# The last pair of a pipelined graph kernel: transposing by TensorE instead of by way of DRAM, a softmax per graph, and own space for y and v

## The chip, the cores and the metric

The kernel runs on one NeuronCore of one Trainium2 chip. The metric is the device time of one execution in microseconds (us). Lengths inside an execution come from the trace of one profiled execution per kernel.

Names of engines in the profile: PE is TensorE (PEld its loads of weights), DVE is VectorE, ACT is ScalarE, POOL is GpSimd, SP is the engine that issues most transfers (883 of 1525 in the trace before).

## The reference

128 graphs of 128 nodes with 512 features, all in fp32, pass through two layers. Cut to what matters:

```python
h = jnp.maximum(_layernorm(x), 0.0)
x = x + _L0_gnn_ref(h, adj, ...)           # layer 0: attention over adj, three hops
h = jnp.maximum(_layernorm(x), 0.0)        # this is "h2" in the kernel
q, k = jnp.split(h @ Wqk, 2, axis=-1)
v = h @ Wv
agg = jnp.einsum('bij,bjd->bid', adj, k * mask)
w = mask / sqrt(512) * jnp.einsum('bid,bid->bi', q, agg)
x = x + jax.nn.softmax(w, axis=1)[:, :, None] * v      # softmax over a graph's nodes
```

The kernel folds Wqk into one matrix, so that layer 1 computes y = h2 times a matrix, v = h2 Wv, agg = adj h2 and the score of a node as the sum of y times agg.

## The kernel before

The graphs are taken in 64 pairs, as a software pipeline: while layer 0 of pair p runs, layer 1 of pair p-1 follows it. Each layer multiplies by a two-by-two block scheme with seven products instead of eight (hence "first to seventh product"; in layer 1 they are run in the order 1, 6, 7, 5, 2, 3, 4, and I call them by their place in that order only where I say so). The products take h2 transposed. The kernel gets that by a trip through DRAM: it stores h2, reads it back by blocks, and lets VectorE transpose blocks of 32 by 32. This is hidden behind the products of other pairs but for two waits of TensorE: 3.29 us for an early pair (at 100.26 us) and 10.45 us for the last.

```python
def by_blocks(h):
    hd = dram.tile([G, P, D], FP, name="hd")
    nc.sync.dma_start(hd.rearrange("g n d -> n g d"), h)
    hv = front.tile([P, G, Q, P], FP, name="hv")
    ...                                   # four loads, one for each 32 partitions
    return hv

def transposed(hv, dst):
    for j in range(G):
        nc.vector.transpose(dst[:, j]..., hv[:, j]...)

def strassen1(p, ahead):                  # layer 1's products of pair p
    product = products(SX2.pop(p), R1)
    yv = late["p"].tile([P, G, 2, 2, HD], FP, name="yv")      # one buffer
    o = ...                               # o[j][nh]: half nh of graph j, y and v side by side
    s = late["p"].tile([P, 3, D], FP, name="s1")
    a, b, c = (ps_m.tile([P, D], FP, name="pm") for _ in range(3))
    product(a, 1, True)
    nc.scalar.copy(s[:, 0], a)
    product(b, 6, True)
    nc.vector.tensor_add(s[:, 1], b, s[:, 0])
    product(c, 7, True)
    agg = [aggregate(p, 0)]
    product(b, 5, False)
    nc.vector.tensor_add(s[:, 2], b, s[:, 0])
    nc.vector.tensor_add(o[1][1], c, s[:, 2])
    ...
    product(a, 2, False)
    nc.scalar.copy(o[0][0], a)
    agg.append(aggregate(p, 1))
    product(b, 3, False)
    nc.vector.tensor_add(o[0][1], b, s[:, 0])
    product(c, 4, False)
    nc.vector.tensor_add(o[1][0], c, s[:, 1])
    return yv, scores(p, yv, agg)         # a score per node, both graphs

def finish(peak, p, yv, ws, pw):          # softmax and result of a pair
    nc.vector.tensor_reduce(peak, pw, AX.X, OP.max, negate=True)
    ...                                   # exponentials on ScalarE, reciprocal, product
    for j in range(G):
        nc.vector.scalar_tensor_tensor(o, yv[:, j, :, 1, :], w[:, 3, j:j + 1], o, ...)
    nc.sync.dma_start(out[p * G:(p + 1) * G].rearrange("b n d -> n b d"), x1)

for p in range(NP + 1):
    if p < NP:
        ...
        strassen0(p, steps)               # layer 0's products; finishes pair p-2 on the way
    else:
        end()                             # finishes pair NP-2
    ...
    if p < NP:
        H2[p] = norm_relu(X1[p], "h2", late["p"])
        hv2 = by_blocks(H2[p])
    ...
    if p > 0:
        yv, w = strassen1(p - 1, p + 2)
    ...
    if p > 0:                             # scores to all partitions, by way of DRAM but for the last
        ends.append((p - 1, yv, w, spread_pair(w, "pw", p < NP)))
    if p < NP:
        X2[p] = late["p"].tile(...)
        transposed(hv2, X2[p]...)
        SX2[p] = left_sums(...)
end()
```

The order of an engine's instructions in the trace (below, the compiled order) follows the source only roughly: in the trace before, VectorE runs the softmax of the pair before (L461, at 2367.68 us) ahead of the last pair's transposes (L279, at 2370.84 us), which the source writes first.

## Time and profile before

| | before |
|---|---|
| median time | 2400.05 us (2398.68 to 2400.31, 3 runs) |
| span of the profiled execution | 2394.7 us |
| TensorE busy | 98% of the span |
| TensorE's longest wait on a product | 10.45 us, at 2361.15 us |
| mean granted clock from 2371.6 to 2385.6 us | 0.88 |

How to read the page: the share of busy time says which engine sets the time; the row of forty digits says where in the execution that holds. A change of the last of 64 pairs can only act in the last slice, so the rest of the reading is a timeline of that slice: look for the stretch without TensorE, see what ended it, and follow that back. The lines are in the prediction below.

### The profile page before, as it was taken

The numbers are of one execution on the slowest core, as the hardware profiler recorded it, in microseconds if no ns is written. First come the engines' busy times: TensorE is split into PE (matmuls) and PEld (weight loads), VectorE is DVE, ScalarE is ACT, GpSimd is POOL, SyncE is SP. The second block draws the span as 40 slices with busy tenths as digits, with TensorE's granted clock in tenths as the row PEclk, the third lists the DMA queues.
The fourth block names the chain that finished last, engine by engine and source line by source line (L and its number), as shares of the span: only waits on it lengthen the run. The fifth ranks groups of instructions, "written<-read, shape, count | busy, mean of one in ns | idle before, by whom it ended". The sixth has DMA issues, their size and how long they took to land.

```text
span 2394.7 us, 27824 instructions
## 1 busy us (share of the span) xinstructions
PE 2338.7 (98%) x8909; PEld 1656.8 (69%) x8909; DVE 1830.6 (76%) x4958; ACT 635.4 (27%) x1557; POOL 369.7 (15%) x646
## 2 busy tenths in 40 slices
PE   5999999999999999999999999999999999999996
PEld 3676676776776776776776776766766766766763
DVE  5777877877877877878878878778778778778764
ACT  3222222222222222222222223223222222222221
POOL 2011111111111111111111111111111111111100
PEclk9999999999999999999999999999999999999998
DMA  8244343343343343343343343442433443443321
GB/s 227 70 112 112 82 115 102 92 114 103 92 106 105 98 106 103 100 106 100 103 106 100 103 106 86 117 106 82 121 105 81 116 110 83 115 112 82 108 67 49
DMA packets 259300, 245.62 MB, mean 103 GB/s; under 512 B 28560, under 2 KB 184336, under 8 KB 259152
## 3 DMA queue, kind: packets, MB, share of 16 engines
q1 hardware_dynamic: 232624, 216.65, 31.9%
q0 software_dynamic: 22304, 25.09, 5.9%
q10 hardware_dynamic: 4224, 2.10, 0.3%
q8 instruction: 70, 1.15, 0.2%
q14 instruction: 78, 0.64, 0.1%
HBM read 142.93 MB, written 100.79 MB: 102 GB/s over the span
## 4 chain that ended last, share of the span: by engine, by line
PE 86%; DVE 6%; DMA 4%; issue 2%; ACT 1%; POOL 0%; DVEq 0%; SPq 0%; POOLq 0%; ACTq 0%
PE pm L367 72%; PE pt L346 8%; PE pt L442 4%; DMA pwd<-pwt 2%; DMA pw<-pwd 1%; PE pt L334 1%; DVE st L224 1%; PE pm L212 1%; PE pt L330 1%; DVE x L279 1%; DVE x L407 0%; DVE sx L354 0%; DVE sx L353 0%; DVE sx L355 0%; DMA pzd<-pzt 0%
## 5 line engine op out<-in xcount | busy, mean ns | idle before, releaser
L367 PE MATMUL pm<-t,sx 128*128 128x256 f32 x2304 | 507.9, 379 | 1.9 <-DVE sx L354 1.9
L367 PEld LDWEIGHTS pm<-t,sx 128*128 128x128 f32 x2304 | 437.6, 190 | 62.1 <-DVE sx L354 2.7
L367 PE MATMUL pm<-b,x 128*128 128x256 f32 x1536 | 363.0, 379 | 0.0
L367 PE MATMUL pm<-f,sx 128*128 128x512 f32 x768 | 352.9, 595 | 4.8 <-DVE s L421 4.8
L367 PEld LDWEIGHTS pm<-b,x 128*128 128x128 f32 x1536 | 282.2, 190 | 59.6 <-issue 29.7
L290 POOL DMA_DIRECT2D pzd<-pzt x126 | 69.9, 556 | 1443.4 <-DVE pzt L287 1443.2
L367 PEld LDWEIGHTS pm<-f,sx 128*128 128x128 f32 x768 | 145.4, 191 | 191.3 <-issue 159.0
L367 PE MATMUL pm<-e,x 128*128 128x512 f32 x512 | 242.9, 597 | 13.7 <-DVE x L279 13.7
L348 ACT COPY x<-pt 128x512 f32<-128x512 f32 x256 | 147.6, 576 | 356.1 <-PE pt L346 356.1
L346 PE MATMUL pt<-tt,h 128*128 128x256 f32 x1024 | 231.5, 379 | 0.0
L262 DVE SCALAR_TENSOR_TENSOR junk<-h,u_bc 128x512 f32<-128x512 f32 x256 | 177.1, 692 | 64.3 <-ACT h L239 52.9
L346 PEld LDWEIGHTS pt<-tt,h 128*128 128x128 f32 x1024 | 194.5, 190 | 26.9 <-ACT tt L335 0.4
L367 PE MATMUL pm<-b,sx 128*128 128x256 f32 x768 | 176.2, 379 | 0.0
L367 PE MATMUL pm<-t,x 128*128 128x256 f32 x768 | 176.2, 379 | 0.0
L367 PEld LDWEIGHTS pm<-e,x 128*128 128x128 f32 x512 | 97.6, 191 | 110.6 <-issue 90.2
L279 DVE STREAM_TRANSPOSE x<-hv 128x512 f32<-128x512 f32 x256 | 166.3, 687 | 7.5 <-DMA hv<-hd 5.6
L307 ACT ACTIVATE s<-s 128x256 f32<-128x256 f32 x63 | 26.2, 416 | 522.8 <-DVE s L305 522.8
L367 PEld LDWEIGHTS pm<-t,x 128*128 128x128 f32 x768 | 145.9, 190 | 19.8
L367 PEld LDWEIGHTS pm<-b,sx 128*128 128x128 f32 x768 | 145.9, 190 | 19.8
L77 POOL DMA_DIRECT2D agb<-in_adj_dram x256 | 152.9, 602 | 18.1 <-DVE aT L319 7.4
L239 ACT ACTIVATE h<-xg,rs 128x512 f32<-128x512 f32 x128 | 97.2, 806 | 184.2 <-DVE rs L236 184.2
L442 PE MATMUL pt<-h,aT 128*128 128x512 f32 x256 | 130.6, 592 | 0.0
(119 smaller groups left out, 2792.7 us busy)
## 6 DMA issues: line engine op xcount, KB each, us to landing
hd<-h SPq DMA_DIRECT2D x128, 512.0 KB, 3.9
hv<-hd SPq DMA_DIRECT2D x512, 128.0 KB, 5.3
xg<-in_x_dram SPq DMA_DIRECT2D x64, 512.0 KB, 3.6
out_dram<-x SPq DMA_DIRECT2D x64, 512.0 KB, 2.8
ag<-in_adj_dram SPq DMA_DIRECT2D x64, 128.0 KB, 2.9
agb<-in_adj_dram POOLq DMA_DIRECT2D x256, 32.0 KB, 4.5
pz<-pzd POOLq DMA_DIRECT2D x63, 128.0 KB, 5.3
pw<-pwd POOLq DMA_DIRECT2D x63, 128.0 KB, 3.3
```

The source lines that it names most:

```text
L77: nc.gpsimd.dma_start(agb[p][c * S32:(c + 1) * S32].rearrange("p g q i -> p (g q) i"), v[c])
L212: nc.tensor.matmul(pm[c], wt[0][:, c * P:(c + 1) * P], wt[1], start=(o == 0), stop=(o == DC - 1))
L224: nc.vector.bn_stats(st, src[:, j, :])
L239: nc.scalar.activation(h[:, j, :], src[:, j, :], AF.Relu, bias=rs[:, 1, j:j + 1], scale=rs[:, 0, j:j + 1])
L262: nc.vector.scalar_tensor_tensor(junk, h[:, j, :], 1.0, u_bc[:, a, :], op0=OP.mult, op1=OP.mult, accum_out=s[:, a * G + j:a * G + j + 1])
L279: nc.vector.transpose(dst[:, j].rearrange("p f (n b) -> p f n b", n=Q), hv[:, j].rearrange("p n (f a) -> p f n a", f=Q))
L290: nc.gpsimd.dma_start(d[j], t[j::S32])
L307: nc.scalar.activation(ex, z, AF.Exp)
L346: nc.tensor.matmul(pt[:, c].rearrange("p k n -> p (k n)"), h[:, j, at:at + P], tt[:, j].rearrange("p k n -> p (k n)"), start=True, stop=True)
L348: nc.scalar.copy(X[p][:, 1:3, j, kh].rearrange("p k c n -> p c k n"), pt)
L367: nc.tensor.matmul(bank[:, :r.shape[-1]], left[i][:, k, c * P:(c + 1) * P], r, start=(first and at == 0), stop=(at == len(chunks) - 1), sk ...
L442: nc.tensor.matmul(pa, AT[p][:, j, :], H2[p][:, j, :], start=True, stop=True)
```

## The change

Its intent: close the hole in front of the last pair's products, and shorten what follows them. Four things change, all for the last pair alone: h2 is stored with its columns reordered and transposed by TensorE; the softmax of the pair before moves behind the last pair's fourth product in program order (number 5); y and v get a buffer of their own, a freed one of layer 0; scores, softmax and store go graph by graph.

```diff
+    def transposed_by_pe(h, dst):
+        for j in range(G):
+            pt = ps_t.tile([P, DC, P], FP, name="pt")
+            for f in range(Q):
+                nc.tensor.transpose(pt[:, f, :], h[:, j, f * P:(f + 1) * P], ident)
+            (nc.vector.tensor_copy if j else nc.scalar.copy)(dst[:, j], pt)
...
-        yv = late["p"].tile([P, G, 2, 2, HD], FP, name="yv")
+        if p + 1 < NP:
+            yv = late["p"].tile([P, G, 2, 2, HD], FP, name="yv")
+        else:
+            yv = front.tile([P, K, G, 2, HC, N], FP, name="x")[:, :2].rearrange(...)
...
         nc.vector.tensor_add(o[1][1], c, s[:, 2])
...
+        if p == NP - 1:
+            end(s[:, 2, :G])
         product(a, 2, False)
...
         nc.vector.tensor_add(o[0][1], b, s[:, 0])
+        w = cols[3 + p % 3]
+        if p == NP - 1:
+            last(p, yv, w, agg, 0)
         product(c, 4, False)
         nc.vector.tensor_add(o[1][0], c, s[:, 1])
-        return yv, scores(p, yv, agg)
+        if p == NP - 1:
+            last(p, yv, w, agg, 1)
+            return
...
+    def last(p, yv, w, agg, j):
+        score(p, yv, w, agg, j)
+        pw = ps_t.tile([P, DC, P], FP, name="pt")
+        spread(pw[:, j, :], w[:, j:j + 1])
+        finish(small.tile([P, G], FP, name="peak"), p, yv, w, pw[:, :G], slice(j, j + 1))
...
-        else:
-            end()
...
-            H2[p] = norm_relu(X1[p], "h2", late["p"])
-            hv2 = by_blocks(H2[p])
+            H2[p] = norm_relu(X1[p], "h2", late["p"], p == NP - 1)
+            if p + 1 < NP:
+                hv2 = by_blocks(H2[p])
...
-            transposed(hv2, X2[p]...)
+            if p + 1 < NP:
+                transposed(hv2, hT2)
+            else:
+                transposed_by_pe(H2[p], hT2)
```

`end(s[:, 2, :G])` puts the maximum of the moved softmax into a corner of a buffer that the sum before it has just read, which keeps the softmax behind that sum.

More of the change, by code (lines that the diff above doesn't have):

```diff
@@ L216, in score_matrix, with norm_relu @@
                 nc.scalar.copy(e[c // HC, nh][:, c % HC, 0, :], pm[c][:, nh * HD:(nh + 1) * HD])
-    def norm_relu(src, name, pool):
+    def norm_relu(src, name, pool, permuted=False):
         mv = small.tile([P, G, 2], FP, name="mv")
@@ L238, in norm_relu, with unpermuted @@
         for j in range(G):
-            nc.scalar.activation(h[:, j, :], src[:, j, :], AF.Relu,
-                                 bias=rs[:, 1, j:j + 1], scale=rs[:, 0, j:j + 1])
-        return h
+            to, at = h[:, j, :], src[:, j, :]
+            if permuted:
+                to, at = unpermuted(to), at.rearrange("p (c f a) -> p c f a", c=DC, f=Q)
+            nc.scalar.activation(to, at, AF.Relu, bias=rs[:, 1, j:j + 1], scale=rs[:, 0, j:j + 1])
+        return h
+    def unpermuted(h):
+        return h.rearrange("p (f c a) -> p c f a", c=DC, f=Q)
     cols = [const.tile([P, S32], FP, name=f"col{i}") for i in range(6)]
@@ L413, in strassen1 @@
         X2.pop(p)
-        yv = late["p"].tile([P, G, 2, 2, HD], FP, name="yv")
+        if p + 1 < NP:
+            yv = late["p"].tile([P, G, 2, 2, HD], FP, name="yv")
+        else:
+            yv = front.tile([P, K, G, 2, HC, N], FP, name="x")[:, :2].rearrange(
+                "p k g h c n -> p (k g h c n)").rearrange("p (j h k d) -> p j h k d", j=G, h=2, k=2)
         o = [[yv[:, j, nh].rearrange("p k d -> p (k d)") for nh in range(2)] for j in range(G)]
@@ L431, in strassen1 @@
         agg.append(aggregate(p, 1))
-        H2.pop(p), AT.pop(p)
         product(b, 3, False)
         nc.vector.tensor_add(o[0][1], b, s[:, 0])
+        w = cols[3 + p % 3]
+        if p == NP - 1:
+            last(p, yv, w, agg, 0)
         product(c, 4, False)
         nc.vector.tensor_add(o[1][0], c, s[:, 1])
-        return yv, scores(p, yv, agg)
+        if p == NP - 1:
+            last(p, yv, w, agg, 1)
+            return
+        for j in range(G):
+            score(p, yv, w, agg, j)
@@ L439, in aggregate @@
+        return yv, w
+    def last(p, yv, w, agg, j):
+        score(p, yv, w, agg, j)
+        pw = ps_t.tile([P, DC, P], FP, name="pt")
+        spread(pw[:, j, :], w[:, j:j + 1])
+        finish(small.tile([P, G], FP, name="peak"), p, yv, w, pw[:, :G], slice(j, j + 1))
     def aggregate(p, j):
         pa = ps_t.tile([P, D], FP, name="pt")
-        nc.tensor.matmul(pa, AT[p][:, j, :], H2[p][:, j, :], start=True, stop=True)
-        return pa
-    def scores(p, yv, agg):
-        w = cols[3 + p % 3]
-        for j in range(G):
-            junk = front.tile([P, D], FP, name="junk", bufs=1)
-            b = p * G + j
-            nc.vector.scalar_tensor_tensor(
-                junk.rearrange("p (k d) -> p k d", k=2), agg[j].rearrange("p (k d) -> p k d", k=2),
-                wscale[:, b:b + 1], yv[:, j, :, 0, :], op0=OP.mult, op1=OP.mult,
-                accum_out=w[:, j:j + 1])
-        return w
@@ L457, in finish, with score @@
-    def finish(peak, p, yv, ws, pw):
+        to, h2 = pa, H2[p][:, j, :]
+        if p == NP - 1:
+            to, h2 = pa.rearrange("p (c f a) -> p c f a", c=DC, f=Q), unpermuted(h2)
+        nc.tensor.matmul(to, AT[p][:, j, :], h2, start=True, stop=True)
+        return pa
+    def score(p, yv, w, agg, j):
+        junk = front.tile([P, D], FP, name="junk", bufs=1)
+        b = p * G + j
+        nc.vector.scalar_tensor_tensor(
+            junk.rearrange("p (k d) -> p k d", k=2), agg[j].rearrange("p (k d) -> p k d", k=2),
+            wscale[:, b:b + 1], yv[:, j, :, 0, :], op0=OP.mult, op1=OP.mult,
+            accum_out=w[:, j:j + 1])
@@ L460, in finish @@
+    def finish(peak, p, yv, ws, pw, graphs=slice(0, G)):
         w = ws[:, :6 * G].rearrange("p (k g) -> p k g", g=G)
-        nc.vector.tensor_reduce(peak, pw, AX.X, OP.max, negate=True)
-        for j in range(G):
+        js = range(G)[graphs]
+        nc.vector.tensor_reduce(peak[:, graphs], pw[:, graphs, :], AX.X, OP.max, negate=True)
+        for j in js:
             ej = front.tile([P, N], FP, name="ej")
@@ L465, in finish @@
                                  accum_out=w[:, 2, j:j + 1])
-        nc.vector.tensor_add(w[:, 3], w[:, 0], peak)
+        w = w[:, :, graphs]
+        nc.vector.tensor_add(w[:, 3], w[:, 0], peak[:, graphs])
         nc.scalar.activation(w[:, 4], w[:, 3], AF.Exp)
@@ L469, in finish @@
         nc.vector.tensor_mul(w[:, 3], w[:, 4], w[:, 5])
-        x1 = X1.pop(p)
-        for j in range(G):
+        x1 = X1[p]
+        for at, j in enumerate(js):
             o = x1[:, j, :].rearrange("p (k d) -> p k d", k=2)
-            nc.vector.scalar_tensor_tensor(o, yv[:, j, :, 1, :], w[:, 3, j:j + 1], o,
+            nc.vector.scalar_tensor_tensor(o, yv[:, j, :, 1, :], w[:, 3, at:at + 1], o,
                                            op0=OP.mult, op1=OP.add)
-        nc.sync.dma_start(out[p * G:(p + 1) * G].rearrange("b n d -> n b d"), x1)
+        nc.sync.dma_start(out[p * G:(p + 1) * G][graphs].rearrange("b n d -> n b d"), x1[:, graphs])
     def begin(p):
@@ L523 @@
         if p < NP:
-            H2[p] = norm_relu(X1[p], "h2", late["p"])
-            hv2 = by_blocks(H2[p])
+            H2[p] = norm_relu(X1[p], "h2", late["p"], p == NP - 1)
+            if p + 1 < NP:
+                hv2 = by_blocks(H2[p])
         if p + 2 < NP:
             norm0(p + 2)
-        if p > 0:
+        if p == NP:
+            strassen1(p - 1, NP)
+        elif p > 0:
             yv, w = strassen1(p - 1, p + 2)
@@ L533 @@
             prepare0(p + 1)
-        if p > 0:
-            ends.append((p - 1, yv, w, spread_pair(w, "pw", p < NP)))
+        if 0 < p < NP:
+            ends.append((p - 1, yv, w, spread_pair(w, "pw", True)))
         if p < NP:
             X2[p] = late["p"].tile([P, G, 2, HC, N], FP, name="x2")
-            transposed(hv2, X2[p].rearrange("p j h c n -> p j (h c) n"))
+            hT2 = X2[p].rearrange("p j h c n -> p j (h c) n")
+            if p + 1 < NP:
+                transposed(hv2, hT2)
+            else:
+                transposed_by_pe(H2[p], hT2)
             a = {(j, kh): X2[p][:, j, kh:kh + 1].rearrange("p k c n -> p k (c n)")
@@ L541 @@
             SX2[p] = left_sums(a, late["p"], "sx2", [1, HD])
-    end()
 _INS = ['x', 'adj', 'nodemask', 'L0_gnn_Wv', 'L0_gnn_bv', 'L0_gnn_aw', 'L0_gnn_ab', 'L0_gnn_Wk',
```

## The prediction

> **What bounds the kernel now.** I began with the first page, to see which engine sets the time and where it pauses: the busy shares, then TensorE's row and its granted clock in forty slices.
>
> ```profile
> PE 2338.7 (98%) x8909; PEld 1656.8 (69%) x8909; DVE 1830.6 (76%) x4958; ACT 635.4 (27%) x1557; POOL 369.7 (15%) x646
> ...
> PE   5999999999999999999999999999999999999996
> ...
> PEclk9999999999999999999999999999999999999998
> ```
>
> TensorE is busy for 98% of 2394.7 us. Only the first and last of the slices (60 us each) show idle time, and in the last the clock falls too. The diff alters only the last of 64 pairs of graphs, so the whole effect must lie in that last slice. Its timeline (start, duration in us, engine, line, output and inputs, count, idle time before) gives the story:
>
> ```profile
> 2356.04 1.52 ACT L239 ACTIVATE h<-x,rs 128x512 f32<-128x512 f32 x2 [0.27 <-PE pt L442]
> ...
> 2357.58 0.38 SPq L269 DMA_DIRECT2D hd<-h  x1
> ...
> 2359.27 1.88 PE L442 MATMUL pt<-h,aT 128*128 128x512 f32 x4
> ...
> 2362.33 1.80 SPq L273 DMA_DIRECT2D hv<-hd  x4
> ...
> 2367.68 0.42 DVE L461 TENSOR_REDUCE peak<-pw 128x2 f32<-128x256 f32 x1 [6.48 <-DMA pw<-pwd]
> ...
> 2369.51 1.41 DVE L473 SCALAR_TENSOR_TENSOR x<-yv,col,x 128x512 f32<-128x512 f32 x2
> ...
> 2370.84 1.30 DVE L279 STREAM_TRANSPOSE x<-hv 128x512 f32<-128x512 f32 x2
> ...
> 2371.60 3.65 PE L367 MATMUL pm<-e,x 128*128 128x512 f32 x4 [10.45 <-DVE x L279]
> ...
> 2375.09 5.31 PE L367 MATMUL pm<-f,sx 128*128 128x512 f32 x12
> ...
> 2390.76 0.39 SPq L475 DMA_DIRECT2D out_dram<-x  x1
> ```
>
> The last h2 is complete at 2357.56. It is stored (landing 4.7 us after issue, in the table of transfers), read back in four blocks (the last issued about 2363.8, landing 2.4 to 3.0 us later, so about 2366.6), and transposed by VectorE only at 2370.84. Those final 4.2 us are not transfer time: VectorE takes its instructions in order, and ahead of the transpose stands the softmax of the pair before, which waits for its own trip through DRAM until 2367.68. TensorE therefore idles 10.45 us. The list of waits confirms this is its largest single wait on the product line (10.4 of 13.7 us):
>
> ```profile
> PE pm L367 <- DVE x L279: 13.7, 2, 10.4
> ```
>
> After the hole comes the final product stage, 2371.60 to 2385.56, then a tail without TensorE work. Busy time by stage (stretch, length, PE, PEld, DVE, ACT, POOL, clock, DMA):
>
> ```profile
> 2361.15:2371.60 10.45, 0.00 (x1) 0.00 (x1) 3.05 (x9) 0.97 (x5) 1.68 (x3) 0.67 0.27 64
> 2371.60:2385.60 14.00, 13.98 (x29) 5.94 (x29) 5.60 (x12) 1.17 (x2) 0.00 (x0) 0.88 0.10 37
> 2385.60:2390.74 5.14, 0.59 (x2) 0.21 (x2) 3.77 (x9) 0.90 (x5) 0.00 (x0) 0.80 0.00 0
> 2390.74:2394.70 3.96, 0.00 (x0) 0.00 (x0) 0.00 (x0) 0.00 (x0) 0.00 (x0) 0.50 0.35 132
> ```
>
> The reader is to see the empty PE column in the first row, a clock of 0.88 in the second, and 5.1 + 4.0 us of softmax and store at the end.
>
> [...]after 10.45 us idle, the first four passes take 2371.60 to 2375.09, 3.49 us, where four warm ones (2380.24 to 2381.95) take 1.71. So 1.78 us of the last stage is a penalty of the hole. [...]the transposes of the weights here record 273 ns, and eight in a row span 1.04 us, as they overlap (starts 0.11 apart). [...]the 0.5 KB transfers of the old score row take 1.6 to 1.9 us, so halving a store cannot halve its landing. [...]
>
> **The change, part by part.**
>
> *Transpose.* Removed: one 512 KB store, four 128 KB loads, two VectorE transposes (1.30). Added: eight TensorE transposes, 8 x 0.11 = 0.9 us, and two copies from PSUM, one on ScalarE (0.59, as the weights' copies and L419) and one on VectorE (0.69, as its other 128x512 operations). I assume they run after the previous pair's final product, which ends at 2359.27 and also releases the single x2 buffer. Then: transposes to 2360.2; the first ScalarE copy ready at about 2360.6; meanwhile the first aggregate fills TensorE to 2361.05. The first product can follow at once, since it needs graph 0 only. The second product needs graph 1: VectorE is busy with the previous pair's scores until 2361.2, then copy 0.69 and three sums at 0.34 spacing, about 2363.1. The first product ends at 2362.8; a 0.3 us stall, or none if the second aggregate is put there.
> TensorE work from 2359.27: 0.9 + two aggregates 2 x 0.86 + seven products of 4 x 0.43 = 12.04, sum 14.66, so the last product ends at about 2374.0, with a small stall 2374.2. Before: 2385.56. Gain here 11.4 (the 10.45 us hole, plus 1.78 of cold clock, less 0.9 of transposes).
>
> *Softmax of the pair before, moved.* It was in the hole; now it follows the fourth product inside the last stage. Its inputs (2367.7) are long there. But its VectorE work, 0.42 + 0.16 + 0.17 + 0.16 + 1.42 = 2.3 us, plus about 0.7 waiting for exponentials, now begins near 2370.4 and reaches 2373.6, in front of the sums and scores of the last products. Own space for y and v is what allows this: the single late buffer would still be read by that softmax.
>
> *Softmax graph by graph.* For graph 1 alone: a narrower maximum (0.42 to about 0.25), one exponential fewer (0.36), one final multiply-add (0.75) instead of two (1.42), a 256 KB store. That would shorten 5.14 us by about 1.2. Against it, both graphs repeat the small instructions, and VectorE is now behind. Counting it in order from 2373.65: L434 0.69, score 0.83, L436 0.69, graph 0's maximum 0.25, score 0.83, to 2377.0; then graph 0's multiply-add falls between, and graph 1's spread, maximum, exponential, reciprocal, product and multiply-add end at about 2380.3. Before, this point was 2390.74: gain 10.4. So 1 us of the 11.4 is given back to the crowded VectorE.
>
> *Store.* Its data moved in some 1.3 us of the last 3.96; half the bytes saves about 0.5. End at about 2380.3 + 3.45 = 2383.7 against 2394.7: **11.0 us less**. Applied to the timed median, 2400.05 - 11.0 = **2389 us**.
>
> **Rivals.** (a) *The order of issue stalls TensorE.* If graph 0's spread is queued ahead of the last product, TensorE waits for a sum and a score: 1.7 to 2.9 us lost, 2391 to 2392. Against: the instructions do not run in source order here (the last pair's aggregates run before its first product, though written after the third), and the spread ran after the last product before. (b) *VectorE becomes the bound of the last stage more strongly*, if it also starts late on the copy for graph 1: 1 to 2 us more, up to 2391. For: it has some 8 us of work after the fifth product, against 5 us of TensorE. (c) *VectorE is not behind*, because the moved softmax runs in earlier gaps: the full 1.2 us of the split is kept, 2387. (d) *The DRAM trip was hidden anyway.* The idle 10.45 us on the engine that ends last says no. (e) *Permuted h2 slows ScalarE or the aggregates*, reading in runs of 32: nothing in the trace before measures it for matmul operands; a copy with just such a permuted output took 586 ns, like the plain ones.
>
> **Range and chances.** Rivals (a) and (b) put it 2 to 3 us higher, (c) 2 us lower; runs of before differ by 1.6 us. Range 2386 to 2393. 2% is 48 us, four times the whole hole, so within 2% is almost certain: 0.98. Faster by more than 2% would need gains outside the last slice, 0.01; slower 0.01.
>
> **What would show it.** In the trace after: no read-back of the last h2; TensorE without a gap over 1 us between the previous pair's last product and the end of the last; its clock near 1.00 there; the last product ending near 2374; eight transposes in about 1 us; VectorE nearly solid from about 2369 to the end; two 256 KB stores, the last issued near 2380. The prediction is wrong if a gap remains before the first product (copy or buffer released late), if TensorE waits at the spread, or if the order of issue changes in earlier pairs and moves the whole run.

## The result, and the profile after

The changed kernel takes **2386.16 us** (median of 6 runs, 2382.4 to 2391.15) against 2400.09 us before (6 runs, 2398.68 to 2400.83). The ratio is 0.9945, with a 95% interval of 0.9932 to 0.9958, so 10 to 16 us less: within 2%, as the prediction expected. A ratio here is the mean time of one kernel's runs over that of the other's of the same rounds, so not quite the ratio of the medians.

The page of the changed kernel, its TensorE row and clock row in forty slices:

```profile
PE   5999999999999999999999999999999999999998
...
PEclk9999999999999999999999999999999999999999
```

Where before the last digits were 6 and 8, they are now 8 and 9. The timeline of the last slice, in the same columns as in the prediction:

```profile
2360.92 1.04 PE L293 MATMUL pt<-ident,h 128*128 128x128 f32 x8
...
2361.55 0.59 ACT L294 COPY x<-pt 128x512 f32<-128x512 f32 x1 [2.35 <-PE pt L293]
...
2361.79 1.02 PE L479 MATMUL pt<-h,aT 128*128 128x512 f32 x2
...
2362.52 0.69 DVE L294 COPY x<-pt 128x512 f32<-128x512 f32 x1
2362.65 1.88 PE L381 MATMUL pm<-e,x 128*128 128x512 f32 x4
...
2364.39 5.42 PE L381 MATMUL pm<-f,sx 128*128 128x512 f32 x12
...
2369.85 0.69 DVE L443 TENSOR_TENSOR s<-pm,s 128x512 f32<-128x512 f32 x1 [2.67 <-PE pm L381]
...
2371.30 0.42 DVE L496 TENSOR_REDUCE s<-pw 128x2 f32<-128x256 f32 x1
2371.36 1.02 PE L479 MATMUL pt<-h,aT 128*128 128x512 f32 x2
...
2373.43 1.41 DVE L509 SCALAR_TENSOR_TENSOR x<-yv,col,x 128x512 f32<-128x512 f32 x2
...
2373.94 1.88 PE L381 MATMUL pm<-f,x 128*128 128x512 f32 x4
...
2379.70 0.75 DVE L509 SCALAR_TENSOR_TENSOR x<-x,col,x 128x512 f32<-128x512 f32 x1
```

The eight transposes, an aggregate and the first product follow each other without a bracket, that is, without idle time before them. L443 is the sum of product 5; from there to the last multiply-add VectorE is busy for 8.80 of 10.60 us; the L479 at 2371.36 is the second aggregate, between products 2 and 3. L496 and the first L509 are the moved softmax, inside the last stage; the second L509 is graph 1's result, the last work before the final store.

To compare traces I use one length throughout. The **mark** is the moment at which TensorE starts its first instruction after the previous pair's last product; the **last stretch** runs from the mark to the end of the span. Before, the mark is at 2359.27 and the last stretch is 2394.7 - 2359.27 = 35.43 us; after, 2360.92 and 2383.5 - 2360.92 = 22.58 us. So the last stretch got 12.85 us shorter, which agrees with the times (0.55% of 2400 us is 13.2). Busy time by stage of the changed kernel's last stretch (columns as in the prediction: stretch, length, PE, PEld, DVE, ACT, POOL, clock, DMA share and rate):

```profile
2360.92:2362.65 1.73, 1.73 (x11) 1.26 (x10) 1.54 (x6) 0.59 (x1) 0.00 (x0) 1.00 0.04 9
2362.65:2375.66 13.01, 13.01 (x31) 5.43 (x29) 7.29 (x17) 2.04 (x7) 1.69 (x3) 1.00 0.05 10
2375.66:2380.45 4.79, 0.78 (x3) 0.27 (x2) 4.32 (x15) 1.21 (x6) 0.00 (x0) 0.93 0.34 127
2380.45:2383.50 3.05, 0.00 (x0) 0.00 (x0) 0.01 (x1) 0.00 (x0) 0.00 (x0) 0.50 0.38 144
```

Set beside the same stages before (the end of the last product is taken as its start plus four passes of 0.43 us, here and in all tails below; the record of the last pass ends 0.16 us later):

| stage of the last stretch | before, us | after, us | gain |
|---|---|---|---|
| mark to end of the last product | 26.12 | 14.74 | 11.38 |
| to the last multiply-add (softmax) | 5.35 | 4.79 | 0.56 |
| to the end (store) | 3.96 | 3.05 | 0.91 |
| last stretch | 35.43 | 22.58 | 12.85 |

TensorE is now busy for 14.74 of 14.74 us up to its last product, at full clock. In the stage after it VectorE is busy for 4.32 of 4.79 us, where before it was 3.77 of 5.14. The store's gain shows in the table of transfers, here the lines of the last stores, first before, then after (size, time from issue to landing):

```profile
out_dram<-x SPq DMA_DIRECT2D x1, 512.0 KB, 2.8
```

```profile
out_dram<-x SPq DMA_DIRECT2D x2, 256.0 KB, 2.0
```

Half the bytes land 0.8 us sooner.

One thing had not been foreseen: the changed kernel's six runs spread over 8.8 us, those of before over 2.2. The mark itself lay 1.65 us later in the changed kernel's trace, though the compiled order of instructions on all five engines is the same up to the last pair (compared instruction by instruction: TensorE's first 8875 of 8909 passes, VectorE's first 4930 of 4958 instructions). Experiment e8 looks at this.

### The profile page after: what moved, and what is told of

Read it like the earlier page. It is cut to its first block, busy times and chain, and to the rows that moved or that the text cites.

```text
span 2383.5 us, 27840 instructions
## 1 busy us (share of the span) xinstructions
PE 2338.9 (98%) x8917; PEld 1656.4 (69%) x8917; DVE 1829.8 (77%) x4961; ACT 636.3 (27%) x1559; POOL 370.9 (16%) x646
## 4 chain that ended last, share of the span: by engine, by line
PE 87%; DVE 5%; DMA 5%; issue 2%; ACT 1%; POOL 0%; SPq 0%; DVEq 0%; POOLq 0%
PE pm L381 73%; PE pt L360 8%; PE pt L479 4%; DMA pwd<-pwt 2%; PE pt L348 1%; DMA pw<-pwd 1%; DVE st L225 1%; PE pt L344 1%; DMA bk_bc<-in_L_gnn_bk_dram 1%; DMA pzd<-pzt 0%; DVE junk L268 0%; DVE x L285 0%; DVE x L421 0%; DMA pz<-pzd 0%; DVE sx L368 0%
## 5 line engine op out<-in xcount | busy, mean ns | idle before, releaser
L479 PE MATMUL pt<-h,aT 128*128 128x512 f32 x256 | 130.7, 592 | 0.0
```

The lines of the kernel that those rows point to most:

```text
L479: nc.tensor.matmul(to, AT[p][:, j, :], h2, start=True, stop=True)
```

## The experiments

All kernels gave the correct result. Chip and rounds are shared within a group: e1 to e4, e5 to e8, e9 to e11, and e12 alone. As the gain of 12.85 us comes from a stretch that repeats to 0.02 us (e8, e11), while whole times scatter by several us, the verdicts on small differences rest on the last stretch.

| kernel | last product starts after the mark, us | last stretch, us | median time, us (runs) | before on that chip, us | ratio, 95% interval |
|---|---|---|---|---|---|
| before | 24.40 | 35.43 | 2400.09 (6) | | |
| the change | 13.02 | 22.58 | 2386.16 (6) | 2400.09 | 0.9932 to 0.9958 |
| e1_pe_only | 13.01 | 23.91 | 2386.64 (4) | 2399.39 | 0.9931 to 0.9960 |
| e2_dram_kept | 21.40 | 32.20 | 2397.53 (4) | 2399.39 | 0.9975 to 1.0004 |
| e3_joint_tail | 13.02 | 24.20 | 2387.90 (4) | 2399.39 | 0.9935 to 0.9964 |
| e4_early_end | 13.02 | 22.31 | 2384.99 (4) | 2399.39 | 0.9920 to 0.9954 |
| e5_warm_fill | 22.51 | 33.58 | 2396.33 (4) | 2395.82 | 0.9984 to 1.0016 |
| e6_pe_spread | 13.63 | 22.88 | 2386.70 (4) | 2395.82 | 0.9942 to 0.9977 |
| e7_halves | 13.65 | 22.73 | 2383.53 (4) | 2395.82 | 0.9931 to 0.9964 |
| e8_change_again | 13.02 | 22.60 | 2384.02 (4) | 2395.82 | 0.9932 to 0.9962 |
| e9_agg_early | 12.89 | 23.42 | 2385.22 (4) | 2397.14 | 0.9930 to 0.9960 |
| e10_tuned | 13.61 | 22.63 | 2383.11 (5) | 2397.14 | 0.9925 to 0.9949 |
| e11_change_5 | 13.02 | 22.59 | 2383.48 (5) | 2397.14 | 0.9927 to 0.9952 |
| e12_tuned2 | 13.03 | 22.11 | 2382.81 (5) | 2397.18 | 0.9926 to 0.9953 |

### e1: the transposes alone

The kernel before with `transposed_by_pe`, the reordered h2 and nothing else of the change.

> The kernel before with only the transposes by TensorE; softmax of the pair before, joint softmax and store, and the shared late buffer stay. I count the last stretch, from the start of TensorE's first instruction after the previous pair's last product to the end of the span: 35.4 us before, 22.6 us after. Theory (the hole is the gain, the rest is small change): the hole vanishes, last stretch 23.5 to 24.3 us, about 11 to 12 us faster than before. Rival (the moved softmax and own space are needed as well, since the softmax of the pair before would still hold VectorE and the late buffer until its scores are back from DRAM): a new wait of 3 us or more on TensorE, last stretch 26 us or more.

Measured: 23.91 us, as the theory had it. The last product starts at 13.01 us, where the whole change has it at 13.02. So the transposes alone bring 11.52 of the 12.85 us, 90%, and the wait that the rival foresaw does not come: with its own transposes out of VectorE's queue, TensorE no longer depends on the softmax of the pair before.

### e2: everything but the transposes

```diff
-            if p + 1 < NP:
-                hv2 = by_blocks(H2[p])
+            hv2 = by_blocks(H2[p])
...
-            if p + 1 < NP:
-                transposed(hv2, hT2)
-            else:
-                transposed_by_pe(H2[p], hT2)
+            transposed(hv2, hT2)
```

The reordering of h2 is taken out with the transposes.

> The changed kernel with the last h2 still transposed by way of DRAM, all else of the change kept. Theory: half of the old hole was the DRAM trip (data back about 7.3 us after the mark) and about 4 us of it the softmax that stood ahead of the transposes on VectorE; the latter is now out of the way, so TensorE idles about 6 us instead of 10.4, the cold clock still costs 1.8 us, last stretch about 30 us. Rival (the hole is all DRAM): idle about 10 us, last stretch 33 to 34 us.

Its timeline around the hole (VectorE's transposes, TensorE's first and second group of passes):

```profile
2371.03 1.30 DVE L285 STREAM_TRANSPOSE x<-hv 128x512 f32<-128x512 f32 x2 [5.81 <-DMA hv<-hd]
...
2371.80 3.78 PE L381 MATMUL pm<-e,x 128*128 128x512 f32 x4 [6.62 <-DVE x L285]
...
2375.37 6.05 PE L381 MATMUL pm<-f,sx 128*128 128x512 f32 x12
...
2381.47 0.69 DVE L443 TENSOR_TENSOR s<-pm,s 128x512 f32<-128x512 f32 x1 [2.67 <-PE pm L381]
```

VectorE now waits for the data itself (5.81 us, released by hv), not behind another pair's softmax, and TensorE's hole is 6.62 us instead of 10.45. That is the split of the hole that the prediction read from the trace: 6.6 us of transfers (with the transposes that follow them), 3.8 us of VectorE's order of issue. The last stretch, 32.20 us, lies between theory (30) and rival (33 to 34); the whole time does not resolve the 3.2 us gained. Besides a hole 0.6 us longer than expected, two terms were missed. The cold clock cost more: the 24 passes of the six products from 2371.80 to 2384.70 take 12.90 us, where before they took 12.07 and warm ones take 10.3 (24 x 0.43), so 2.6 us instead of 1.8. The granted clock shows where the difference lies (here in two stretches of 3.41 us; the clock is the third number from the end):

```profile
2370.03:2373.44 3.41, 1.64 (x2) 0.84 (x3) 2.37 (x5) 0.00 (x0) 0.00 (x0) 0.50 0.13 28
2373.44:2376.85 3.41, 3.41 (x5) 1.35 (x4) 0.45 (x2) 0.58 (x1) 0.00 (x0) 0.50 0.00 0
```

The clock is 0.50 in both and 1.00 after 2376.85. The products start at 2371.80, and TensorE runs slow for 5.05 us. Before, the clock was 0.50 from 2364.75 to 2374.99; the products started at 2371.60 and ran slow for 3.39 us. Why the clock came back 5.05 us after the start of the products in one trace and 3.39 us after it in the other is not shown; no run here varied the moment of that start alone.

And the tail is 1.0 us longer than the change's (5.80 us from the end of the last product to the last multiply-add, against 4.79). Most of this comes from the aggregates: here both run before the hole and none stands between products 2 and 3, so VectorE gets the sum of product 5 (L443) only 4.95 us before the last product ends, in the change 5.81 us before. This build's compiled order also has the scores of both graphs together; from the first sum after the moved softmax to the last multiply-add it takes 5.85 us, the change 5.69.

### e3: one softmax and one store for both graphs

```diff
-        if p == NP - 1:
-            last(p, yv, w, agg, 0)
...
-            last(p, yv, w, agg, 1)
+            finish(small.tile([P, G], FP, name="peak"), p, yv, w, spread_pair(w, "pw", False))
```

> The changed kernel with the last pair's scores, softmax and store taken for both graphs together, as before. Theory: the split is worth 1.2 to 1.5 us (about 0.4 us of softmax, 0.9 us of store), last stretch 23.8 to 24.1 us. Rival (my prediction's: VectorE is so far behind that the split brings only the store's half microsecond): 23.0 us.

Measured: 24.20 us, 1.6 us more than the change and 0.1 above the expected range. The split by graph is worth 1.6 us, more than the 0.5 that the prediction's view of a late VectorE would have left.

### e4: no own space, the softmax of the pair before ahead of the last products

```diff
-        if p + 1 < NP:
-            yv = late["p"].tile([P, G, 2, 2, HD], FP, name="yv")
-        else:
-            yv = front.tile(...)
+        if p == NP - 1:
+            end()
+        yv = late["p"].tile([P, G, 2, 2, HD], FP, name="yv")
...
-        if p == NP - 1:
-            end(s[:, 2, :G])
```

> The changed kernel with the y and v of the last pair in the shared late buffer again and the softmax of the pair before written ahead of the last products, so that it may run as soon as its scores are back; transposes by TensorE and graph-by-graph softmax kept. Theory: own space is worth nothing, as the old y and v are read before the new ones must be written; last stretch 22.0 to 22.7 us, the same as the change. Rival (own space is what makes the overlap possible): 1 to 3 us longer, with a wait of VectorE or ScalarE on the late buffer.

Measured: 22.31 us, 0.27 less than the change. The wait that the rival named is there, and costs nothing:

```profile
2370.88 0.42 DVE L492 TENSOR_REDUCE peak<-pw 128x2 f32<-128x256 f32 x1 [2.33 <-DMA pw<-pwd]
...
2374.23 0.58 ACT L446 COPY yv<-pm 128x512 f32<-128x512 f32 x1 [1.93 <-DVE x L505]
```

The mark is at 2362.29 here. The maximum starts when the scores come back, 8.6 us after the mark; in the change it starts at 10.4 us (2371.30 - 2360.92), held back by the sum that it was tied to. ScalarE's copy into the shared buffer waits 1.93 us for the old multiply-adds, but TensorE does not need that bank again, and the last product starts at 13.02 as before. So the own space and the later place of the softmax bring nothing here; starting the softmax sooner is slightly better.

### e5: the hole kept, the clock kept warm

The kernel before with eleven products of h2 that nobody reads, in front of the last pair's first product:

```diff
+        if p == NP - 1:
+            h = fill.pop()
+            pf = ps_t.tile([P, D], FP, name="pt")
+            for i in range(11):
+                nc.tensor.matmul(pf, h[:, i % G, :P], h[:, i % G, :], start=(i == 0), stop=(i == 10))
         product(a, 1, True)
```

> The kernel before with eleven idle products of h2 (nobody reads them) queued on TensorE in its 10.4 us hole, 9.5 us of work, so that the clock stays up; everything else waits as before. Theory: the hole's second cost is the cold clock, 1.8 us; the first pass after the hole starts at the same distance from the mark (12.3 us), the last stage's products take 12.1 us instead of 13.9, last stretch 33.6 us instead of 35.4. Rival (the slow passes come from the start itself, not from the clock): last stretch unchanged at 35.4 us.

The first pass after the hole starts 12.10 us after the mark (12.33 before), and what follows runs at full clock, by timeline and by stage:

```profile
2369.12 1.99 PE L367 MATMUL pm<-e,x 128*128 128x512 f32 x4 [0.78 <-DVE x L279]
```

```profile
2369.30:2381.50 12.20, 12.18 (x29) 5.09 (x29) 5.45 (x12) 1.17 (x2) 0.00 (x0) 1.00 0.11 43
```

Four passes in 1.99 us instead of 3.65, a clock of 1.00 instead of 0.88, a last stretch of 33.58 us: 1.85 us less, 1.8 expected. Of this, 1.66 us lie in the products themselves (10.41 us from the start of the first to the start of the last, 12.07 before); the rest is their start, 0.23 us earlier. The whole time does not resolve this (2396.33 us against 2395.82, its four runs spread over 8.5 us).

### e6 and e7: trying to relieve VectorE

e6 spreads the scores of the pair before by TensorE and lets its softmax start at once:

```diff
+        if p == NP - 1:
+            end()
         product(b, 5, False)
...
-        if p == NP - 1:
-            end(s[:, 2, :G])
...
-            ends.append((p - 1, yv, w, spread_pair(w, "pw", True)))
+            ends.append((p - 1, yv, w, spread_pair(w, "pw", p < NP - 1)))
```

> The changed kernel with the scores of the pair before spread by TensorE as well (two transposes more) instead of by way of DRAM, and its softmax free to run as soon as they are there, so that it falls into VectorE's idle time between the second and the fifth product. Theory (after the hole is gone, the end is set by VectorE's queue from the fifth product on): last stretch 21.7 to 22.2 us instead of 22.6. Rival (the end is set by TensorE and the fixed chain after the last product, VectorE's moved softmax costs nothing): 22.6 to 22.8 us, as TensorE has two transposes more.

```profile
2367.32 0.29 PE L101 MATMUL pt<-ident,col 128*128 128x128 f32 x1
2367.45 1.04 PE L293 MATMUL pt<-ident,h 128*128 128x128 f32 x8
...
2368.72 1.12 PE L381 MATMUL pm<-e,x 128*128 128x512 f32 x2 [0.24 <-ACT x L294]
...
2369.68 0.27 PE L101 MATMUL pt<-ident,col 128*128 128x128 f32 x1
```

Measured: 22.88 us, just above the rival's range. The two spreads split TensorE's sequence, with a wait of 0.24 us, and the last product starts 0.6 us later; the tail gets shorter by only 0.3. (In e6 and e7 the mark is the first spread, before which TensorE idles 0.2 us; counted from the end of the previous pair's last product, the last stretches are 23.08 and 22.92 us.)

e7 adds that the seventh and the fourth product of the last pair are computed in halves of 256 columns into two banks, y first, so that graph 1's score can start before v is done, and that graph 0's softmax is queued behind graph 1's score:

```diff
-        product(c, 4, False)
-        nc.vector.tensor_add(o[1][0], c, s[:, 1])
+            product(cs[0], 4, False, halves[0])
+            nc.vector.tensor_add(o[1][0][:, :HD], cs[0][:, :HD], s[:, 1, :HD])
+            product(cs[1], 4, False, halves[1])
+            last(p, yv, w, agg, 1, lambda: nc.vector.tensor_add(
+                o[1][0][:, HD:], cs[1][:, :HD], s[:, 1, HD:]))
```

> As e6_pe_spread, and the last pair's seventh and fourth product computed in two halves of 256 columns in two banks, y first, so that graph 1's score starts before the v half is done; graph 0's softmax is queued behind graph 1's score. Theory (the score of graph 1 heads the final chain): 0.5 to 0.9 us less than e6, last stretch 20.9 to 21.5 us. Rival (the narrower passes and the extra sums eat it): the same as e6.

Measured: 22.73 us, 0.15 us less than e6, which is too little to be read (see e8), and the theory's number is missed by more than 1 us. The tail did shrink (from the end of the last product to the last multiply-add 4.3 us, 4.5 in e6, 4.8 in the change), but TensorE's last product starts at 13.65 us, as in e6.

### e8 and e11: the change again

> The changed kernel once more, unaltered, on the same chip as the others: shows how well the last stretch repeats. Theory: the scatter of the times (2382 to 2391 us) arises ahead of the last stretch, so the last stretch repeats within 0.2 us of 22.58 while the mark moves by a microsecond or more. Rival (the last stretch itself varies): off by 1 us or more.

> The changed kernel unaltered, on the same chip and in the same number of rounds as e10. Theory: last stretch 22.6 us within 0.1 for the third time; its time 1 to 1.4 us above e10's, which the scatter of some 3 us of the part ahead may hide. Rival: the last stretch moves by more than 0.2 us, so differences of that size between experiments mean nothing.

Measured: 22.60 and 22.59 us, after 22.58; the last product starts at 13.02 us in all three. So differences of 0.2 us between last stretches can be read. The mark, on the other hand, lay at 2360.92, 2361.00 and 2357.21 us, and over all the traces between 2357.0 (e5) and 2367.3 (e6). Taking the start of each pair's propagation (the group of passes of pt<-tt,h) against that in the trace before, e6 is late by 0.74 us at the first pair, 3.5 at the ninth, 4.7 at the 29th, 7.85 at the last, in instructions that are the same. So the scatter of the times arises ahead of the last stretch, in steps spread over the whole execution. For a part of them the profile names a releaser: TensorE waits for a sum of layer 1 on VectorE (L421 before, L439 in e6), seven times in either trace, 4.8 us in all before (1.17 us of it at 367.31) and 6.9 us in e6 (1.48 us of it at 1820.85). Why VectorE is later there in one execution than in another, and what makes the rest, is open. That the change scatters more than the kernel before is not shown either: over all rounds the change ran from 2381.5 to 2391.2 us (15 runs) and the kernel before from 2395.1 to 2402.1 (38 runs), 9.6 and 7.0 us.

### e9: the second aggregate early

```diff
         product(a, 1, True)
         nc.scalar.copy(s[:, 0], a)
+        if p == NP - 1:
+            agg = [aggregate(p, j) for j in range(G)]
         product(b, 6, True)
```

> The changed kernel with one edit: the last pair's second aggregate is written ahead of the second product, where TensorE otherwise stalls 0.7 us, as my prediction had assumed it. It ought to end TensorE's last product 0.7 us sooner (it starts 12.3 us after the mark instead of 13.0). Theory (from the fifth product on VectorE's queue sets the end, so TensorE's gain is lost there; the scores of both graphs then stand together in VectorE's order): last stretch 22.6 to 23.2 us, no better than 22.6. Rival (TensorE still sets the end): 21.9 us.

This expectation contained a misreading. The timeline of the change has 0.69 us of idle time before a load of weights ahead of product 6, and I took it for a stall of TensorE. The passes themselves have no gap there: the first product starts at 2362.65 and takes 1.72, the next starts at 2364.39. So the last product could not move by 0.7 us, and it moved by 0.13. The theory's direction was confirmed, more strongly than expected: 23.42 us, 0.84 longer than the change and above the range of 22.6 to 23.2, though TensorE ends no later.

```profile
2369.44 0.69 DVE L446 TENSOR_TENSOR s<-pm,s 128x512 f32<-128x512 f32 x1 [2.67 <-PE pm L381]
...
2375.55 0.74 DVE L490 SCALAR_TENSOR_TENSOR junk<-pt,wscale,x 128x512 f32<-128x512 f32 x1
...
2376.35 0.32 PE L101 MATMUL pt<-ident,col 128*128 128x128 f32 x1 [1.80 <-DVE junk L490]
```

The mark is at 2359.78. The sum of product 5 (L446) starts 9.66 us after it, in the change (2369.85) 8.93 us. From there on VectorE works through its queue, and the first score starts at 15.8 instead of 14.6 us. At the last multiply-add it is 0.89 us later than in the change: 0.73 of that is the later start, 0.16 the compiled order, which in this build too has both sums and then both scores (5.85 instead of 5.69 us, as in e2). The aggregate behind product 5 is thus worth some 0.7 us by itself: it costs TensorE 0.13 us and lets VectorE start 0.73 us sooner.

### e10 and e12: a combination

e10 combines the early aggregate, the softmax of the pair before set free (`end()` with its own small buffer) and the halves of e7.

> The second aggregate early as in e9, the softmax of the pair before free to run as soon as its scores are back (scores still by way of DRAM, since e6 showed that TensorE's spread costs more than it brings), and the seventh and fourth product in two halves, y first, with graph 0's softmax queued behind graph 1's score, as in e7. Theory: VectorE is clear when the last product's y half is done; last product starts at 12.3 us, ends at 14.1, and 7.3 us follow as in e7: last stretch 21.2 to 21.6 us, 1.0 to 1.4 us less than the change. Rival (VectorE stays behind): 22.3 us or more.

Measured: 22.63 us, no better than the change; the rival's "22.3 or more" holds. The multiply-add of the free softmax was put ahead of the sum of product 5, and product 3, which accumulates in the same bank, waited 0.45 us for that sum; the last product started at 13.61 us.

e12 puts the aggregate back:

> e10 with the second aggregate back where the change has it (between the second and the third product). e9 and e10 showed TensorE without a gap in the change, so moving the aggregate ahead only delays the fifth product and with it VectorE. Theory: the softmax of the pair before starts when its scores land, about 8.6 us after the mark, and is done by 12.4, before the third product; last product starts at 13.0 as in the change, the final chain from graph 1's score on takes 3.9 us and the store 3.1, as in e7: last stretch 22.0 to 22.2 us, 0.4 to 0.6 less than the change. Rival (the halves cost TensorE what they save): 22.6 us.

```profile
2369.74 1.41 DVE L531 SCALAR_TENSOR_TENSOR x<-yv,col,x 128x512 f32<-128x512 f32 x2
...
2372.12 0.69 DVE L464 TENSOR_TENSOR x<-pm,s 128x512 f32<-128x512 f32 x1 [0.97 <-PE pm L381]
```

Measured: 22.11 us, in the expected range, 0.47 less than the change. VectorE is done with the old softmax and idles 0.97 us before the third product's sum, that is, it waits for TensorE again. This is the shortest last stretch of all, and 13.3 us below the kernel before. Its time (2382.81 us) is the lowest median too, but half a microsecond is far inside the scatter of the times; that e12 beats the change rests on the traces alone.

## Why the prediction was right

**The time.** 2389 us was predicted, with a range of 2386 to 2393; 2386.16 us was measured over six runs, 0.16 us above the lower end. The last stretch was to lose 11.0 us and lost 12.85.

**The hole and its two causes: right.** e2 confirms the reading that only part of the hole was transfer: 6.62 us remain when nothing else stands ahead of the transposes. The hole goes with the transposes alone (e1).

**The cold clock: right.** 1.78 us read from the passes, 1.85 us measured with the hole filled, of which 1.66 us in the products (e5). That the same loss can be 2.6 us (e2) was not foreseen.

**TensorE's new sequence: right to 0.2 us.** Eight transposes take 1.04 us, the copies 0.59 and 0.69 as assumed. The last product ends 14.74 us after the mark, predicted 14.7 to 14.9. (Its gain of 11.4 sets the end before, 2385.56, which is that of the last record, against an end after by passes of 0.43 us; set alike, the sum gives 11.2, and 11.38 was measured.) The feared stall of the second product did not come.

**The tail: the term that was mis-sized.** The prediction gave 6.1 us from the end of the last product (2374.2) to the last multiply-add (2380.3), "1 us of the 11.4 is given back to the crowded VectorE"; the trace has 4.79. Counted from the mark, the last multiply-add was put at 21.03 us and came at 19.53, so 1.50 us sooner. Two terms were too long. The first is where the second aggregate stands. The sum took it to run ahead of product 5 (it was to fill TensorE's gap there), and had VectorE begin with that product at about 2369, 9.7 us after the mark. In the compiled order it stands between products 2 and 3, and VectorE begins at 8.93 us. e9 builds TensorE's order that I had assumed: VectorE begins at 9.66 us, and the last multiply-add comes at 20.42 us. So 0.7 to 0.8 of the 1.50 us are this step. The second is the chain after the moved softmax: 6.65 us in the sum (2373.65 to 2380.3), 5.69 us in the trace (2374.76 to 2380.45), so 1.0 us: the sums and scores took 2.9 us instead of 3.3, what follows them 2.75 instead of 3.3. Against both, the stretch up to the end of the moved softmax took 0.3 us longer than counted. The mechanism, VectorE's queue setting the end from product 5 on, holds (e9, e12).

**The store: mis-sized by 0.4 us.** 3.45 us predicted, 3.05 measured; half the size saved 0.8 us of landing, not 0.5.

**Own space for y and v: wrong in its meaning.** "Own space for y and v is what allows this" is true of the place that the change gave to the softmax, but e4 shows that neither the place nor the space earns anything: without them the last stretch is 22.31 us.

**The rivals.** (a) Graph 0's spread did not stand ahead of the last product; it ran after it in every build. (b) VectorE was late by 0.84 us only in e9. (c) In the change VectorE's lateness costs some 0.3 to 0.5 us (e4, e12), so the truth lay between (b) and (c), nearer to (c). (d) The trip was not hidden: e1 alone brings 11.52 us. (e) Reordered h2 costs nothing: the aggregates take 592 ns in the change as before, and the activations that write h2 798 to 817 ns in both.

**Luck.** In the times of the first comparison the change gained 13 to 14 us rather than 11. The prediction stayed inside its range because the range allowed for it, not because the tail was right; and with single runs from 2382.4 to 2391.15 us, three of six below 2386, it is luck that the median lies 0.16 us inside.

## What to carry to other kernels

When a kernel is bound by one engine at 98%, look at the ends of the execution, and ask of a hole not only which transfer it waits for but what stands ahead in the queue of the engine that takes the data: here 3.8 of 10.4 us were order of issue. Once the hole was closed, the next bound of this kernel was the engine that drains the last results, VectorE (busy for 4.32 of the 4.79 us after the last product), and what counted was when it gets its input (an aggregate placed behind product 5 instead of ahead of it: 0.84 us). Before crediting a whole change, build its parts: one of its four parts brought 90%; two, taken out together in e4, brought nothing.
